# A two-layer graph attention kernel: the first lookup table in node order, its loads and stores on ScalarE, the second layer's indices from VectorE

## The chip, the cores and the metric

One core of a Trainium2 chip. The time is the device time of one execution in microseconds (us), as the median of several runs. TensorE is PE in the profile, VectorE DVE, ScalarE ACT, GpSimd POOL, SyncE SP.

## The reference

Eight batches of 2048 nodes with 64 values each, and one adjacency matrix of 2048 x 2048 integers. Layer 1 has four heads, layer 2 one.

```python
mask = graph + jnp.eye(N, dtype=graph.dtype) > 0
h = jnp.einsum('bnc,hdc->bhnd', x, Wh)
out_h = _gat_layer(h, mask[None, None], bh[None, :, None, :])   # scores h h^T, masked, softmax, times h, plus b
cat = jnp.transpose(out_h, (0, 2, 1, 3)).reshape(B, N, H * D)
z = jax.nn.leaky_relu(cat, negative_slope=0.2)
h2 = jnp.einsum('bnk,dk->bnd', z, Wo)
out2 = _gat_layer(h2, mask[None], bo)
z2 = jax.nn.leaky_relu(out2, negative_slope=0.2)
mu = jnp.mean(z2, axis=-1, keepdims=True)
var = jnp.mean(jnp.square(z2 - mu), axis=-1, keepdims=True)
out = (z2 - mu) * jax.lax.rsqrt(var + LN_EPS) * gamma + beta
x = _layernorm(x + out, axis=-1)
```

The adjacency is sparse: the chance of an edge between two nodes falls with both numbers, so nodes with low numbers have many neighbours and the others few.

## The kernel before, in words

The kernel uses the sparsity. The first 32 nodes (`HUB`) are computed against all nodes. The other 2016 are put into 168 sets (`NS`) of 12 (`SET`), and for each set a list of at most 128 neighbours of any of its members is made. A set is then worked on with the 128 rows of its list only, which GpSimd gathers from a table in device memory (`indirect_dma_start`, L817): `table1` holds x of all batches (2080 bytes a node), `table2` the layer-2 values. A node's number alone does not say where it stands in a table: the members of a set stand next to each other, 12 rows a set, and member 0 of the sets comes in blocks of 24 (`FLIP`) in reversed order of the blocks. One tile `index` (128 list places x 168 sets) holds row numbers for both tables.

**First stage.** SP loads the adjacency in pieces of 120 rows x 1024 (10 sets; a load of 10 rows, at times cut in two, for the members 0, L694, and one of 110 rows for the rest, L695). GpSimd turns a piece into zeros and ones (L700). TensorE multiplies by powers of two, so that bit k of a column says whether member k of the set has that neighbour; VectorE adds the column's row number (`number`, L731): key = bits x 2048 + number. Then the largest 128 keys of each set are searched eight at a time (`pick`, L758 and L760), transposed, and cut into row number (`index`, L788) and bits (`mask`, L801). An entry that is no neighbour gets 2048 added, which the gather leaves out as out of bounds.

Beside this a loop over 16 tiles of 128 nodes (`for i in range(NB)`, L979) works on the hub nodes: `load_x(i + 4)` loads a later tile of x (two transfers, L474; the tiles 0 to 3 on ScalarE's queue, the rest on SP's), `save_x(i)` stores tile i to `table1` (L479, on ScalarE's queue, one transfer for each run of rows that the table's order leaves together, 33 for all tiles), `hub_scores(i)` makes scores on TensorE (L615), subtracts the mask on VectorE (L618) and takes the exponential on ScalarE (L620), `turn_x(i + 1)` transposes the next tile (ScalarE copies it to `xT`, L608), `hub_values(i - 1)` multiplies by the values (L631). At i = 2 and 6 the keys of the first 60 sets are made, and from i = 6 on four steps of `pick` follow in each iteration. Each queue works in the order in which its instructions are recorded; a wait of a transfer on ScalarE's queue holds ScalarE's later instructions too.

The transfers that SP and ScalarE issue are counted by eight semaphores, given out in turn over both queues in the common order of the recorded program. A transfer that takes a semaphore again waits until that semaphore's earlier transfer has landed, if its engine has not seen that yet.

**Second stage.** A loop over 84 pairs of sets (`for i in range(-4, NG + 3)`, L1125) runs layer 1: gather five pairs ahead (L1153, L817), transpose (L538), scores (L847), mask (L852), exponential, values (L872), normalise (L879, L880), bias and leaky ReLU (L544, L549), projection for layer 2 (L906, L911), rows of `table2` stored (L920, L923). Small jobs for later are put in between by iteration; the list `ahead_of_second` holds jobs that prepare layer 2 (clearing buffers, `link` at L1060), one every second iteration from i = 60 on.

**Third stage.** Layer 2 over groups of four sets: gather from `table2` with the same `index`, transposes, scores, values (L1275), two layer norms, and the stores of the result (L1358).

Of the kernel before, what the change touches and what calls it, by code (L numbers as in the profile page):

```python
# [31 lines left out]
I32 = mybir.dt.int32  # L32
# [4 lines left out]
OP = mybir.AluOpType  # L37
# [7 lines left out]
HUB = 32  # L45
SET = 12
# [313 lines left out]
def fast_kernel(ctx: ExitStack, tc: tile.TileContext, x, adj, Wh, bh, Wo, bo, gamma, beta, out, flag):  # L360


    nc = tc.nc
    B, N, C = x.shape
    H, D, _ = Wh.shape
    P = 128
# [7 lines left out]
    NS = (N - HUB) // SET  # L374
# [7 lines left out]
    HALFN = N // 2  # L382
    NHB = (NS + S10 - 1) // S10
    FLIP = 24
    REST = HUB + NS
    assert NS * SET == N - HUB and NS % FLIP == 0 and FLIP % 8 == 0 and HUB == 32 and Q * HUB == P

    const = ctx.enter_context(tc.tile_pool(name="const", bufs=1))
# [15 lines left out]
    def rows_tile(name):  # L404
        return rowp.tile([P, Q, PW], F32, tag="rows", name=name)
# [11 lines left out]
    share = [const.tile([P, n], F32, name=f"share{k}") for k, n in enumerate([HALFN, HALFN, HALFN, 512, 512, 2 * 264])]  # L417
# [10 lines left out]
    table1 = dram.tile([N, ROW], F32, name="table1")  # L428
# [7 lines left out]
    ownh = const.tile([P, Q * HUB], F32, name="ownh")  # L436
    keysi = const.tile([P, NS], I32, name="keysi")
    index = const.tile([P, NS], I32, name="index")
    mask = const.tile([P, NS, M], U8, name="mask")
    maskh = const.tile([P, NB, HUB * H], U8, name="maskh")  # L440
    maskt = const.tile([P, NHB + 1, HUB], U8, name="maskt")
# [8 lines left out]
    xrow = {}  # L450

    def flipped(s0, ns):

        runs = []
        while ns:
            n = min(ns, FLIP - s0 % FLIP)
            runs.append((s0, HUB + (NS // FLIP - 1 - s0 // FLIP) * FLIP + s0 % FLIP, n))
            s0, ns = s0 + n, ns - n
        return runs

    def in_order(table, a, b):

        sets = table[HUB:, :].rearrange("(s k) c -> k s c", k=SET)
        runs = [(0, HUB, table[:HUB, :])]
        runs += [(n0, n0 + n, sets[0, s0:s0 + n]) for s0, n0, n in flipped(0, NS)]
        runs += [(HUB + k * NS, HUB + (k + 1) * NS, sets[k]) for k in range(1, SET)]
        return [(max(a, n0), min(b, n1), dst[max(a, n0) - n0:min(b, n1) - n0]) for n0, n1, dst in runs if max(a, n0) < min(b, n1)]

    def load_x(i):
        t = xrow[i] = rows_tile(f"x{i}")  # L470
        nc.vector.memset(t[:, :, 0:PW:PW - 1], 1.0)
        for p in range(2):
            queue = nc.scalar if i < 4 else nc.sync
            queue.dma_start(out=t[:, :, 1 + p * D:1 + (p + 1) * D],  # L474
                                in_=x[p::2, i * P:(i + 1) * P, :].rearrange("q n c -> n q c"))

    def save_x(i):
        for a, b, dst in in_order(table1, i * P, (i + 1) * P):
            nc.scalar.dma_start(out=dst, in_=xrow[i][a - i * P:b - i * P].rearrange("n q c -> n (q c)"))  # L479

    NCH = HALFN
    in_round = [min(FIRST, NS - FIRST * r) for r in range(NR)]
    pieces = [(r, t, m) for r in range(NR) for t in range((in_round[r] + S10 - 1) // S10) for m in range(2)]
    load_x(0)
    hubraw = [early.tile([HUB, NCH], I32, tag="raw", name=f"hubraw{k}", bufs=3) for k in range(2)]
    for k in range(2):
        nc.sync.dma_start(out=hubraw[k], in_=adj[0:HUB, k * NCH:(k + 1) * NCH])
    for r in range(2):
        nc.sync.dma_start(out=wnat[half(r)], in_=Wh.rearrange("h d c -> d h c"))
    nc.sync.dma_start(out=wos, in_=Wo)  # L490
    load_x(1)
    with nc.allow_non_contiguous_dma(reason="a few hundred bytes of parameters"):
        nc.gpsimd.dma_start(out=bhp, in_=bh.rearrange("(q e) d -> (e d) q", e=2))
# [12 lines left out]
    for k in range(SET):  # L506
        nc.gpsimd.affine_select(out=d, in_=d, pattern=[[0, 3], [-1, 10]], base=-10 * k, channel_multiplier=1,
                                compare_op=OP.not_equal, fill=float(1 << k))
    number = share[2].bitcast(U16).rearrange("p (h c) -> p h c", h=2)
    nc.gpsimd.iota(number[:, :, :HUB // 2], [[1, 2], [2, HUB // 2]], base=0, channel_multiplier=0)  # L510
    nc.gpsimd.iota(number[:, :, HUB // 2:REST // 2].rearrange("p h (b c) -> p h b c", c=FLIP // 2),
                   [[SET, 2], [-FLIP * SET, NS // FLIP], [2 * SET, FLIP // 2]], base=HUB + SET * (NS - FLIP), channel_multiplier=0)
    nc.gpsimd.iota(number[:, :, REST // 2:].rearrange("p h (k c) -> p h k c", k=SET - 1),
                   [[SET, 2], [1, SET - 1], [2 * SET, NS // 2]], base=HUB + 1, channel_multiplier=0)
    load_x(2)
    load_x(3)

# [296 lines left out]
    def gather(table, s, layer, new):  # L814
        t = rows[layer, s] = new(f"g{layer}_{s}")
        bound = {} if layer == 2 and s < 36 else dict(bounds_check=N - 1, oob_is_err=False)
        nc.gpsimd.indirect_dma_start(out=t.rearrange("n q c -> n (q c)"), out_offset=None, in_=table,  # L817
                                     in_offset=bass.IndirectOffsetOnAxis(ap=index[:, s:s + 1], axis=0), **bound)

    def own_rows(m):  # L820

        t = held["x", m] = work.tile([P, 2 * GM], F32, tag="xo", name=f"xo{m}", bufs=2)
        to = t.rearrange("c (s q k) -> c s q k", s=4, q=Q)
        nc.gpsimd.tensor_copy(to[:, :, :, 1:], xT[:, :, REST:].rearrange("c q (k s) -> c s q k", s=NS)[:, 4 * m:4 * m + 4])
        n0 = flipped(4 * m, 4)[0][1]
        nc.gpsimd.tensor_copy(to[:, :, :, 0], xT[:, :, n0:n0 + 4].rearrange("c q s -> c s q"))
# [187 lines left out]
    for g in range(LOOK - 2):  # L1014
        for j in range(2):
            gather(table1, 2 * g + j, 1, rows_tile)
# [19 lines left out]
    sets = [list(range(4 * u, min(4 * u + 4, NS))) for u in range(NU)]  # L1036
    bd = [t.rearrange("p (k q n) -> p k q n", k=4, q=Q) for t in (share[2][:, :512], share[2][:, 512:], share[4])]
    es2 = [t.rearrange("p (b k n) -> p b k n", b=2 * Q, k=4) for t in share[:2]]
# [4 lines left out]
    def spread_own(u):  # L1043

        w = len(sets[u])
        for p in range(2):
            src = own[half(p), :, sets[u][0] * SET:(sets[u][0] + w) * SET]
            nc.scalar.copy(bd[u % 3][half(p), :w, :, 16 * p:16 * p + SET], src.rearrange("c q (k n) -> c k q n", k=w))
# [6 lines left out]
    def clear_ends():  # L1055
        for k in range(2):
            nc.vector.memset(esh[k][:, Q * 2 * HUB:], 1.0)
        nc.vector.memset(es2[0][:, :, :, 24:], 1.0)

    def link():  # L1060
        nc.vector.tensor_scalar(index[:, :36], index[:, :36], N - 1, None, OP.bitwise_and)
        nc.vector.tensor_scalar(linked, mask.rearrange("p s (k h) -> p s k h", h=H)[:, :, :, 0], 0.0, None, OP.is_equal)

    W2 = D + 2
# [46 lines left out]
    def hub_step(k, sp):  # L1111
# [3 lines left out]
        if 0 < k <= NHB + 1:  # L1115
            hub_values2(k - 1)

    ahead_of_second = ([clear_own] + [lambda t=t: nc.vector.memset(t, 0.0) for t in bd + es2] + [clear_ends, link] +
                       [lambda u=u: spread_own(u) for u in range(3)])

    ready, done = FIRST, FIRST
# [3 lines left out]
    for i in range(-4, NG + 3):  # L1125
# [15 lines left out]
        if 0 <= i + 2 < NG:  # L1141
            t = held["T", 1, i + 2] = work.tile([P, 2, 512], F32, tag="xTg", name=f"xTg{i + 2}", bufs=3)
# [11 lines left out]
        if NG - LOOK <= i < NG - 1:  # L1154
            for j in range(2):
                k = 2 * (i - NG + LOOK) + j
                hub_block(k, rows_tile(f"gh{k}"))
        if i + 6 < NG and i % 2 == 0 and i >= -2:
            own_rows((i + 6) // 2)
        if i >= 60 and i % 2 == 0 and ahead_of_second:  # L1160
            ahead_of_second.pop(0)()
        if i % 2 == 0 and 0 <= (i - 30) // 2 <= NV:
            load_own((i - 30) // 2)
# [252 lines left out]
    k = 9  # L1416
    for u in range(-3, NU + 5):
# [12 lines left out]
        if 0 <= u < NU:  # L1430
            a = u % 2
# [10 lines left out]
        if 0 <= u + 1 < NU:  # L1442
            turn_scores(u + 1)
            a = (u + 1) % 2
# [49 lines left out]
```

## Time and profile before

| | us |
|---|---|
| median of 3 timed runs | 1020.71 (1017.41 to 1027.33) |
| the profiled execution, its own time | 892.68 |
| its span from first to last instruction | 890.9 |
| first exponential of the tile loop (L620) starts | 46.42 |
| last exponential of the tile loop starts | 122.31 |
| first gather of layer 1 (L817) starts | 130.98 |
| last gather of layer 1 starts | 576.0 |
| first gather of layer 2 starts | 611.1 |

The profiled execution was shorter than the timed runs by 128 us. The profile's page gives busy times, which overlap; the chain that ended last is followed back from the last instruction, step by step to what released it. In a row of a timeline come the start, the time it took, the engine, the line, what is written and read, and in brackets how long the engine had stood idle and what ended that. "ACTq" and "SPq" are instructions that issue a transfer; their time is that of the issue, not of the data.

### The profile page before, as it was taken

The numbers are of one execution on the slowest core, as the hardware profiler recorded it, in microseconds if no ns is written. First come the engines' busy times: TensorE is split into PE (matmuls) and PEld (weight loads), VectorE is DVE, ScalarE is ACT, GpSimd is POOL, SyncE is SP. The second block draws the span as 40 slices with busy tenths as digits, with TensorE's granted clock in tenths as the row PEclk, the third lists the DMA queues.
The fourth block names the chain that finished last, engine by engine and source line by source line (L and its number), as shares of the span: only waits on it lengthen the run. The fifth ranks groups of instructions, "written<-read, shape, count | busy, mean of one in ns | idle before, by whom it ended". The sixth has DMA issues, their size and how long they took to land.

```text
span 890.9 us, 42340 instructions
## 1 busy us (share of the span) xinstructions
PE 729.4 (82%) x18079; PEld 644.2 (72%) x18079; DVE 592.2 (66%) x1358; ACT 502.6 (56%) x1038; POOL 503.2 (56%) x709
## 2 busy tenths in 40 slices
PE   2266657899999999999999999986998888888830
PEld 2254545788889889889898888875887787887720
DVE  2136962788978778775556566552249989998882
ACT  2032313566656666666666666662567778787720
POOL 5234338386445456556566666504777777777501
PEclk9998977999999999999999999999799999999965
DMA  7377746344223334444444444435975666766510
GB/s 118 117 215 187 208 151 167 91 141 112 79 78 91 95 97 128 121 124 133 127 136 131 129 125 126 115 97 151 301 219 164 191 181 185 204 187 182 172 45 25
DMA packets 82419, 125.70 MB, mean 141 GB/s; under 512 B 35440, under 2 KB 51672, under 8 KB 82222
## 3 DMA queue, kind: packets, MB, share of 16 engines
q0 software_dynamic: 27168, 69.09, 28.4%
q1 hardware_dynamic: 48088, 48.36, 18.6%
q10 hardware_dynamic: 6966, 5.45, 2.3%
q8 instruction: 145, 2.38, 1.1%
q14 instruction: 52, 0.43, 0.1%
HBM read 124.98 MB, written 18.48 MB: 161 GB/s over the span
## 4 chain that ended last, share of the span: by engine, by line
PE 52%; DVE 16%; DMA 13%; issue 6%; SPq 5%; ACT 4%; POOL 2%; ACTq 0%; POOLq 0%; DVEq 0%
PE o L872 10%; PE s L847 9%; PE bank L538 7%; DMA raw<-in_adj_dram 6%; PE cat L832 5%; PE cat L557 3%; PE o L889 3%; SPq L1358 3%; DMA rows<-table,index 3%; PE cat L906 3%; PE t L538 2%; PE cat L916 2%; DVE st_s L1309 2%; DVE y_s L1329 2%; DMA table<-x 2%
## 5 line engine op out<-in xcount | busy, mean ns | idle before, releaser
L817 POOL DMA_INDIRECT g<-table,index x168 | 178.0, 1060 | 163.5 <-PE o L872 133.7
L817 POOL DMA_INDIRECT rows<-table,index x168 | 178.1, 1060 | 55.5 <-issue 23.2
L852 DVE TENSOR_TENSOR e<-s,mask 128x768 f32<-128x768 f32 x84 | 80.3, 955 | 87.7 <-PE s L847 87.6
L544 ACT ACTIVATE z<-cat,bhp 128x192 f32<-128x192 f32 x168 | 61.4, 416 | 80.3 <-PE cat L557 80.3
L872 PE MATMUL o<-g,e 128*64 128x65 f32 x2688 | 100.5, 226 | 4.7 <-issue 4.5
L538 PE MATMUL bank<-ident,g 128*128 128x128 f32 x672 | 101.5, 275 | 0.7 <-DVE keysi L786 0.6
L1390 ACT COPY xts<-t 128x1024 f32<-128x1024 f32 x84 | 81.1, 1010 | 33.1 <-PE t L538 31.5
L872 PEld LDWEIGHTS o<-g,e 128*64 128x64 f32 x2688 | 87.3, 139 | 16.1 <-issue 6.2
L847 PE MATMUL s<-y,xTg 64*64 64x48 f32 x5376 | 97.6, 221 | 1.3 <-DVE share L731 1.2
L847 PEld LDWEIGHTS s<-y,xTg 64*64 64x64 f32 x5376 | 86.9, 135 | 15.6 <-issue 15.1
L538 PE MATMUL t<-ident,rows 128*128 128x128 f32 x672 | 86.3, 279 | 10.1 <-DMA rows<-table,index 9.4
L1144 ACT COPY xTg<-bank 128x512 f32<-128x512 f32 x168 | 90.2, 596 | 0.6 <-PE bank L538 0.6
L538 PEld LDWEIGHTS t<-ident,rows 128*128 128x128 f32 x672 | 76.5, 144 | 14.2 <-issue 6.3
L700 POOL TENSOR_SCALAR a<-raw 120x1024 bf16<-120x1024 int32 (+1 forms) x34 | 37.8, 1113 | 81.2 <-DMA raw<-in_adj_dram 55.2
L538 PEld LDWEIGHTS bank<-ident,g 128*128 128x128 f32 x672 | 80.9, 142 | 3.3 <-DVE keysi L786 1.2
L838 ACT COPY y<-cat 128x384 f32<-128x384 f32 x80 | 41.0, 513 | 73.5 <-PE o L889 36.2
L859 ACT ACTIVATE e<-e,shifts 128x768 f32<-128x768 f32 x84 | 81.0, 964 | 2.4 <-DVE e L852 2.4
L879 DVE RECIPROCAL rall<-o 64x8 f32<-64x8 f32 x168 | 34.4, 205 | 51.4 <-PE o L872 50.1
L832 PE MATMUL cat<-xo,gram 128*128 128x192 f32 x320 | 65.9, 328 | 0.7 <-issue 0.7
L880 DVE TENSOR_TENSOR osb<-o,rall 128x512 f32<-128x512 f32 x84 | 58.1, 692 | 2.9
L620 ACT ACTIVATE e<-e,shifts 128x1024 f32<-128x1024 f32 x16 | 18.4, 1149 | 73.2 <-DVE e L618 36.1
L832 PEld LDWEIGHTS cat<-xo,gram 128*128 128x128 f32 x320 | 53.3, 201 | 1.6 <-issue 1.4
(193 smaller groups left out, 1446.1 us busy)
## 6 DMA issues: line engine op xcount, KB each, us to landing
raw<-in_adj_dram SPq DMA_DIRECT2D x32, 440.0 KB
table<-xb SPq DMA_DIRECT2D x22, 256.0 KB
xr_s<-table SPq DMA_DIRECT2D x21, 256.0 KB
table<-rowt SPq DMA_DIRECT2D x166, 24.4 KB
xb<-in_x_dram SPq DMA_DIRECT2D x168, 22.0 KB
out_dram<-y_s SPq DMA_DIRECT2D x160, 22.0 KB
x<-in_x_dram SPq DMA_DIRECT2D x24, 128.0 KB
g<-table,index POOLq DMA_INDIRECT x168
```

The source lines that it names most:

```text
L538: nc.tensor.transpose(tp[:, q * P:(q + 1) * P], rows[:, q, 1:1 + P], ident)
L544: nc.scalar.activation(z[:, hp], cat[:, :, hp * n:(hp + 1) * n], AF.Identity, bias=bhp[:, hp:hp + 1], scale=1.0)
L817: nc.gpsimd.indirect_dma_start(out=t.rearrange("n q c -> n (q c)"), out_offset=None, in_=table, in_offset=bass.IndirectOffsetOnAxis(ap=ind ...
L832: nc.tensor.matmul(cat[:, k, 2 * GM:2 * GM + n], gram[:, g % 2 * 2 + k, :], held["x", g // 2][:, :n], start=True, stop=True)
L838: nc.scalar.copy(held["y", g // 2][:, :n, g % 2 * 2:g % 2 * 2 + 2], cat[:, :, 2 * GM:2 * GM + n].rearrange("p a n -> p n a"))
L847: nc.tensor.matmul(sp[half(r), p, (q * 2 + j) * M:(q * 2 + j + 1) * M], xt[half(p), j, q, half(r)], y[half(p), (j * Q + q) * M:(j * Q + q ...
L852: nc.vector.tensor_tensor(e[:, :16 * M].rearrange("p (a q n) -> p a q n", a=2, q=Q), sp[:, :, :8 * M].rearrange("p a (q n) -> p a q n", q= ...
L859: nc.scalar.activation(e[:, :16 * M], e[:, :16 * M], AF.Exp, bias=shifts[:, 0:1], scale=1.0)
L872: nc.tensor.matmul(op[half(p), j, o0:o0 + K1], e[:, c0:c0 + 64], rw[j][:, q, sums(p)], start=True, stop=True)
L880: nc.vector.tensor_tensor(osb, v[:, :, :, 1:K1], r.unsqueeze(3).to_broadcast([P, 4, 2, D]), OP.mult)
L1144: nc.scalar.copy(t[:, k, :], bank[k])
L1390: nc.scalar.copy(t, tp)
```

## The change

`table1` is stored in the order of the node numbers, each tile of 128 nodes by one transfer on ScalarE's queue; `in_order` is gone. `number` is then the node's number itself, made by one iota. `index` therefore points into `table1` only, and layer 2, whose `table2` keeps the order of the sets, gets a tile `index2`, which VectorE works out from `index` by comparing the node number with the bounds of member classes and blocks (25 instructions on 128 x 168 integers). These stand as five jobs at the head of `ahead_of_second`, which now starts at i = 50. All tiles of x are loaded from ScalarE's queue.

```diff
     index = const.tile([P, NS], I32, name="index")
+    index2 = const.tile([P, NS], I32, name="index2")
...
-    def in_order(table, a, b):
-
-        sets = table[HUB:, :].rearrange("(s k) c -> k s c", k=SET)
-        runs = [(0, HUB, table[:HUB, :])]
-        runs += [(n0, n0 + n, sets[0, s0:s0 + n]) for s0, n0, n in flipped(0, NS)]
-        runs += [(HUB + k * NS, HUB + (k + 1) * NS, sets[k]) for k in range(1, SET)]
-        return [(max(a, n0), min(b, n1), dst[max(a, n0) - n0:min(b, n1) - n0]) for n0, n1, dst in runs if max(a, n0) < min(b, n1)]
-
     def load_x(i):
         t = xrow[i] = rows_tile(f"x{i}")
         nc.vector.memset(t[:, :, 0:PW:PW - 1], 1.0)
         for p in range(2):
-            queue = nc.scalar if i < 4 else nc.sync
-            queue.dma_start(out=t[:, :, 1 + p * D:1 + (p + 1) * D],
+            nc.scalar.dma_start(out=t[:, :, 1 + p * D:1 + (p + 1) * D],
                                 in_=x[p::2, i * P:(i + 1) * P, :].rearrange("q n c -> n q c"))
 
     def save_x(i):
-        for a, b, dst in in_order(table1, i * P, (i + 1) * P):
-            nc.scalar.dma_start(out=dst, in_=xrow[i][a - i * P:b - i * P].rearrange("n q c -> n (q c)"))
+        nc.scalar.dma_start(out=table1[i * P:(i + 1) * P, :], in_=xrow[i].rearrange("n q c -> n (q c)"))
...
-    nc.gpsimd.iota(number[:, :, :HUB // 2], [[1, 2], [2, HUB // 2]], base=0, channel_multiplier=0)
-    nc.gpsimd.iota(number[:, :, HUB // 2:REST // 2].rearrange("p h (b c) -> p h b c", c=FLIP // 2),
-                   [[SET, 2], [-FLIP * SET, NS // FLIP], [2 * SET, FLIP // 2]], base=HUB + SET * (NS - FLIP), channel_multiplier=0)
-    nc.gpsimd.iota(number[:, :, REST // 2:].rearrange("p h (k c) -> p h k c", k=SET - 1),
-                   [[SET, 2], [1, SET - 1], [2 * SET, NS // 2]], base=HUB + 1, channel_multiplier=0)
+    nc.gpsimd.iota(number, [[1, 2], [2, HALFN]], base=0, channel_multiplier=0)
...
-                                     in_offset=bass.IndirectOffsetOnAxis(ap=index[:, s:s + 1], axis=0), **bound)
+                                     in_offset=bass.IndirectOffsetOnAxis(ap=(index if layer == 1 else index2)[:, s:s + 1], axis=0), **bound)
...
+    node, late_sets, blocks = [share[5][:, k * NS:(k + 1) * NS].bitcast(I32) for k in range(3)]
+
+    def node_steps():
+        nc.vector.tensor_scalar(node, index, N - 1, None, OP.bitwise_and)
+        nc.vector.tensor_scalar(late_sets, node, float(REST), None, OP.is_ge)
+        nc.vector.tensor_scalar(blocks, node, float(HUB + FLIP), None, OP.is_ge)
+        nc.vector.scalar_tensor_tensor(index2, late_sets, float(SET * (NS - FLIP)), index, OP.mult, OP.add)
+
+    def count(into, first, step, js):
+        for j in js:
+            nc.vector.scalar_tensor_tensor(into, node, float(first + step * j), into, OP.is_ge, OP.add)
+
+    def set_order():
+        nc.vector.scalar_tensor_tensor(index2, late_sets, float(1 - NS * SET), index2, OP.mult, OP.add)
+        nc.vector.scalar_tensor_tensor(index2, blocks, float(-2 * FLIP * SET), index2, OP.mult, OP.add)
+        nc.vector.tensor_scalar(blocks, node, float(HUB), None, OP.is_ge)
+        nc.vector.tensor_scalar(node, node, float(SET - 1), float(SET * (NS - FLIP) - HUB * (SET - 1)), OP.mult, OP.add)
+        nc.vector.tensor_tensor(node, node, blocks, OP.mult)
+        nc.vector.tensor_tensor(index2, index2, node, OP.add)
+
     def link():
-        nc.vector.tensor_scalar(index[:, :36], index[:, :36], N - 1, None, OP.bitwise_and)
+        nc.vector.tensor_scalar(index2[:, :36], index2[:, :36], N - 1, None, OP.bitwise_and)
...
-    ahead_of_second = ([clear_own] + [lambda t=t: nc.vector.memset(t, 0.0) for t in bd + es2] + [clear_ends, link] +
+    ahead_of_second = ([node_steps, lambda: count(late_sets, REST, NS, range(1, 6)), lambda: count(late_sets, REST, NS, range(6, SET - 1)),
+                        lambda: count(blocks, HUB, FLIP, range(2, NS // FLIP)), set_order, clear_own] + [lambda t=t: nc.vector.memset(t, 0.0) for t in bd + es2] + [clear_ends, link] +
                        [lambda u=u: spread_own(u) for u in range(3)])
...
-        if i >= 60 and i % 2 == 0 and ahead_of_second:
+        if i >= 50 and i % 2 == 0 and ahead_of_second:
```

## The prediction

> **What bounds the kernel now.** I read the page first (busy shares, the 40 slices, the chain), then busy time by stretch, then the timelines of ACT, DVE and SP over the first 165 us, because all three named edits act there or on what it leaves behind. From the page:
>
> ```profile
> span 890.9 us, 42340 instructions
> PE 729.4 (82%) x18079; PEld 644.2 (72%) x18079; DVE 592.2 (66%) x1358; ACT 502.6 (56%) x1038; POOL 503.2 (56%) x709
> ```
>
> By stretch (us, then busy us of each engine, granted clock, DMA share, GB/s):
>
> ```profile
> 36.00:76.00 40.00, 22.03 (x432) 16.98 (x432) 9.92 (x13) 11.34 (x14) 17.33 (x63) 1.00 0.78 213
> 76.00:131.00 55.00, 34.10 (x655) 26.37 (x653) 47.04 (x125) 14.11 (x17) 19.29 (x42) 0.84 0.59 171
> 131.00:390.00 259.00, 242.00 (x6208) 215.15 (x6212) 194.90 (x519) 158.28 (x362) 151.28 (x227) 0.97 0.40 111
> ```
>
> Up to 76 us no engine is busy; the stretch waits. From 76 to 131 us VectorE works 47 of 55 us. From 131 us on TensorE works 94%. So a gain can only come from the first 76 us (the second stretch then starts earlier at its old length), and work added to VectorE after 131 us costs only where it makes TensorE wait. In the first stretch ScalarE stands before its first exponentials:
>
> ```profile
> 36.14 10.17 ACTq L479 DMA_DIRECT2D table<-x  x5
> 46.42 1.15 ACT L620 ACTIVATE e<-e,shifts 128x1024 f32<-128x1024 f32 x1 [21.61 <-DMA table<-x]
> ...
> 51.40 1.15 ACT L620 ACTIVATE e<-e,shifts 128x1024 f32<-128x1024 f32 x1 [3.36 <-DMA table<-x]
> ```
>
> The operand of the first exponential was done at 31.07 (VectorE, L618, 29.84 + 1.23). The bracket is the idle time and what ended it: five stores of one x tile, queued ahead on ScalarE. The chain of waits says what the last of the five waited for:
>
> ```profile
> 41.04 4.95 DMA raw<-in_adj_dram
> 46.01 2.89 DMA table<-x
> ```
>
> The wait is not for the tile: in the built program the transfers of SP and ACT take eight semaphores in turn in one common order, so each is issued only when the eighth before it has landed. An adjacency load of 110 rows issued at 41.04 lands at 45.99 and frees the store. After that the loop of 16 tiles turns at 4.17 us (exponential 1.15, xT copy 0.57, scores 1.1, subtract 1.23) until VectorE's keys and top-8 searches fill it:
>
> ```profile
> 76.36 2.47 DVE L731 SCALAR_TENSOR_TENSOR share<-pk,share 32x1024 f32<-32x1024 f32 x2 [2.19 <-PE pk L742]
> ```
>
> In the long stage an iteration takes 5.00 us, and VectorE has room in it. Two places show how much: at 473.67 three extra instructions (0.77 us) before L549, and at 550 the step `link`.
>
> ```profile
> 476.23 0.27 DVE L1051 MEMSET share<- 128x256 f32 x1
> 476.54 0.50 DVE L1053 COPY share<-ownh 64x128 f32<-64x128 f32 x2
> ...
> 477.91 0.27 DVE L920 TENSOR_TENSOR rowt<-cat,bob 96x128 f32<-96x128 f32 x1
> 478.67 0.96 DVE L852 TENSOR_TENSOR e<-s,mask 128x768 f32<-128x768 f32 x1 [0.48 <-PE s L847]
> ...
> 550.10 1.28 POOL L951 TENSOR_TENSOR xb<-xb,bet 128x512 f32<-128x512 f32 x1 [3.52 <-DMA table<-rowt]
> 550.15 1.27 DVE L1061 TENSOR_SCALAR index<-index 128x36 int32<-128x36 int32 x1
> 551.34 1.31 DVE L1062 TENSOR_SCALAR maskh<-mask 128x2016 uint8<-128x2016 uint8 x1
> ...
> 553.57 0.50 ACT L838 COPY y<-cat 128x384 f32<-128x384 f32 x1 [3.02 <-DVE rowt L920]
> ...
> 554.55 0.92 PE L557 MATMUL cat<-otb,whT 64*64 64x96 f32 x16 [1.96 <-ACT otb L896]
> ```
>
> In the first, L920 ends 4.51 us after its iteration's L852 instead of 3.39 (406.34 to 409.73), and the next L852 still comes 5.00 us later: 1.1 us of delay are free. In the second L920 is 2.4 us late, ScalarE's copy L838 waits for it, TensorE stands 1.96 us, and the two iterations from 547.67 to 561.27 take 13.60 instead of 10.0.
>
> **What the Trainium skill says.** DMA: Bandwidth & Descriptors, section Issuing engines are not separate DMA queues: transfers of ScalarE and SyncE run on the same 16 engines, so a change of queue saves issue time only. I take the moved loads' data time as unchanged; no view here contradicts it. Same page, Anatomy of one DMA — SWDGE (gpsimd) path: a fixed cost of about 2 us per transfer, mostly the receipt, stated for transfers that GpSimd issues. The trace has the same for SP's: 10 rows of 4 KB issued at 15.44 take 1.93 us in the chain. Same page, Why a DMA increments its semaphore by 16 and not by 1: a transfer runs on the largest number of engines up to 16 that divides its rows, so 24 rows use 8 and 128 rows 16; no view shows engines singly. SBUF — State Buffer, section Who interferes with whom: VectorE in a two-port mode (tensor_scalar can enter it) and GpSimd block each other for a whole instruction. The trace agrees: L1061 on 36 columns took 1.27 us beside POOL's L951, where L788 on 60 columns took 0.19.
>
> **The change part by part.** The profiled execution took 892.68 us around a span of 890.9; the median of the timed runs is 1020.71, 128 us more, and nothing in the profile places that. I work on the profiled execution and carry the difference over in us.
>
> *Stores.* 33 stores become 16. The first tile's five become one, the second's four become one. *Loads of x4 to x15.* 24 issues leave SP and go to ScalarE, each pair ahead of that iteration's store and exponential. SP's next adjacency loads are no longer behind them; ScalarE goes from 41 to 48 issues (33 + 8, then 16 + 32), in the loop three an iteration. At the median 0.48 us for a load (L474) and 0.36 for a store (L479) that is 1.3 us, and ScalarE idles 2.55 us between its xT copy and the next exponential: hidden, as long as no semaphore holds them.
>
> Now the semaphores, by the built program's order. Iteration 0: the two loads of x4 stand where the first two stores stood and wait for the same landings (36.12 and 39.42, from the stores' issue at 36.14 and 39.44); the store stands where the third stood, issued at 40.03. First exponential about 40.5 for 46.42: 6 us earlier. Iteration 1: the loads of x5 wait for the 10-row load issued at 41.92, and the store for the 110-row load issued at 42.48; with 6 us for that (49.20 to 55.20 in the chain) it lands at 48.7, exponential about 49.1 for 51.40: 2.3 left. Iteration 2: the loads of x6 wait for piece 4's 110 rows, free to issue at 46.0 instead of 46.66, landing 5.5 us later; exponential about 52.5 for 55.58. Iteration 3, after the keys' 2.5 us on VectorE: 58.7 for 61.68. With turns of 4.17 the second keys then start near 73.4 for 76.36, **3.0 us earlier**. What can give it back: without the x loads SP's pieces come closer together, the common order has 26 transfers in the four iterations from x8 to x12 (17 before), and eight in flight at 6.5 an iteration allow a landing time of 8/6.5 x 4.17 = 5.1 us; pieces land in 4.6 to 6 us here. So one or two of the loads x8 to x10 should hold ScalarE for about a microsecond. I take half: **-1.5 us** at the first gather. Bounds: -13 (ScalarE never held: the first exponential at 31.1, the seventh six turns and one pair of keys later, and the second keys 2.2 us behind it as now: 31.1 + 25.0 + 2.5 + 2.2 = 60.8; I put 63, an estimate, because the twelfth piece, converted at 66.36 now, has to be in by then) and +9 (0.75 us lost in each of 12 iterations).
>
> *From 76 to 131 us.* VectorE's list is unchanged; ScalarE waits 3.3 us in each turn for VectorE, which covers three issues. 0. *Iota.* One for three (0.15 + 0.31 + 1.74 us before), and POOL then waits 2.75 us for the adjacency anyway: 0. *Layer-1 gathers.* Same 168, same rows in another order, issued five iterations ahead; TensorE's transposes have no wait for them worth a row: 0. *Layer-2 gathers* read the same table through `index2`, with rows in the order of nodes instead of sets; they make 2.8% of the chain, 25 us, so a tenth longer would be 2.5 us. I take 0 and keep 0 to +2.5.
>
> *VectorE's 25 instructions at i = 50, 52, 54, 56, 58* (4, 5, 5, 5, 6), all on 128x168 and each on the result before it. Nearest row: the 128x168 int32 TENSOR_TENSOR at 119.49, its successor at 119.85, so 0.36 us each: 1.44, three times 1.80, 2.16; 9.0 us in all. They stand ahead of L549, as `link` does: behind them L549, L911, L920, then ScalarE's L838 and L896, then TensorE's L557. With 1.1 us free each time: 0.34 + 3 x 0.70 + 1.06 = **+3.5 us**. Bounds: 0 (TensorE slower than in this profile would leave more room) and +10 (two tensor_scalar instructions blocked 1.1 us by POOL's L951, and half the price of `link`'s second slow iteration each time). The rest of that list (`clear_own` to `spread_own`) keeps its iterations from i = 60.
>
> Sum: -1.5 + 3.5 = +2.0, 894.7 for 892.68; on the median **1022.7**.
>
> **Rivals.** *A, within 1%* (the above). *B, faster:* adjacency transfers were the pacer and fewer transfers in the common order let both loads and stores flow. For it: 50% of the chain up to 76 us are adjacency transfers, 12.8% stores. Against: the first six pieces go one by one to 34 us, untouched. Its time is the lower bound of the first stretch with the index work hidden: -13, 1007.7. *C, slower:* ScalarE's queue becomes the bound. Its exponential and xT copy, and so TensorE's scores and VectorE's subtract, stand behind loads that wait for adjacency pieces. It decides once pieces land later than about 5.1 us in the 4.17-us turns, 6.1 in turns of 4.95. For it: landings of 5.74 at 92.02 and 6.00 at 49.20. Against: VectorE's pace leaves 3.3 us from 78 us on. Price +9 with +3.5 from VectorE: 1033.2. *That the change doesn't do what it says:* the moved loads could wait for the same landings that SP waited for, so that the first stretch keeps its length and only the index work is seen, +3.5: 1024.2, inside A.
>
> **How the numbers follow.** A 0.45, B 0.30, C 0.25. One per cent, 10 us, is about what a measurement of this kernel tells from no change (the three runs span 1017 to 1027). A's own range is -4 to +8, 1017 to 1029. The range reaches to B and C and a little past, 1005 to 1036. B and C are each taken as whole beyond 1%, A as whole within it: faster 0.30, same 0.45, slower 0.25.
>
> **What would show it.** Right: first exponential near 40.5, second near 49, the second keys near 73 to 76, first gather (130.98 before) within 129 to 131; the iterations at i = 50 to 58 at 5.3 to 6.1 us with ScalarE's L838 copy ended by VectorE. Wrong: a first gather before 122 (B), or ScalarE's exponentials ended by transfers of x over several microseconds in many tiles (C), or any difference after 615 us.

## The result and the profile after

The change takes 1031.58 us at the median, the kernel before 1021.99 on the same chip (16 runs each): ratio 1.008, 95% interval 1.0058 to 1.0103, so 8.2 us slower, between 5.9 and 10.5. The forecast was 1022.7 with "within 1%" as the likeliest outcome; that is where it fell, at the slow edge (0.8%, and the interval reaches just past 1%), and the sum of the prediction (+2.0) is too small by some 6 us.

The profiled execution of the change took 1023.52 us. That of the kernel before took 892.68 us, which is what this kernel takes on a faster chip, as the first experiment shows; so the two pages are not subtracted from each other, and stretches are compared only where a run allows it. The page of the changed kernel begins:

```profile
span 1021.7 us, 42335 instructions
PE 772.5 (76%) x18079; PEld 667.6 (65%) x18079; DVE 605.3 (59%) x1383; ACT 507.1 (50%) x1038; POOL 499.5 (49%) x707
```

VectorE has 25 instructions more, as written, and 13.1 us more busy time; 10.5 of these are the 25 (mean 0.42 us). The timeline of ScalarE in the tile loop after the change, in the same columns as the one shown of before (the exponential is now line 607, loads of x line 466, stores line 470):

```profile
37.47 4.50 ACTq L466 DMA_DIRECT2D x<-in_x_dram  x2
42.25 0.35 ACTq L470 DMA_DIRECT2D table<-x  x1
42.72 1.15 ACT L607 ACTIVATE e<-e,shifts 128x1024 f32<-128x1024 f32 x1 [19.63 <-DMA x<-in_x_dram]
...
49.21 0.93 ACTq L466 DMA_DIRECT2D x<-in_x_dram  x2
50.82 0.35 ACTq L470 DMA_DIRECT2D table<-x  x1
51.21 1.15 ACT L607 ACTIVATE e<-e,shifts 128x1024 f32<-128x1024 f32 x1 [6.88 <-DMA x<-in_x_dram]
```

The stores no longer hold the first exponential (42.72 for 46.42), but the loads do: two of them take ScalarE's queue 4.50 us, because the second waits for an earlier transfer, the adjacency load of 110 rows that SP issued at 35.89. At the second tile nothing is left of the gain (51.21 for 51.40). VectorE's second keys, at 77.50, come no earlier than before (76.36 in the profile shown of before, 77.55 in a second one):

```profile
77.50 2.46 DVE L718 SCALAR_TENSOR_TENSOR share<-pk,share 32x1024 f32<-32x1024 f32 x2 [2.19 <-PE pk L729]
```

The chain of waits between 30 and 80 us names the loads outright; two of its pieces show how long a load took whose semaphore the next transfer on ScalarE's queue needed:

```profile
51.26 7.07 DMA x<-in_x_dram
58.36 5.50 DMA x<-in_x_dram
```

The first gather starts at 130.53, for 130.98 before. In the long stage the timeline around the third job of the index work (i = 54) shows where time goes (L907 makes rows of layer 2, L825 and L883 are ScalarE's copies, L544 the projection, L859 the values):

```profile
464.69 2.49 DVE L1057 SCALAR_TENSOR_TENSOR share<-share 128x168 int32<-128x168 int32 x5
467.10 0.55 DVE L536 SCALAR_TENSOR_TENSOR z<-z 128x384 f32<-128x384 f32 x1
467.74 0.28 DVE L907 TENSOR_TENSOR rowt<-cat,bob 96x128 f32<-96x128 f32 x1
468.10 0.50 ACT L825 COPY y<-cat 128x384 f32<-128x384 f32 x1 [3.01 <-DVE rowt L907]
468.49 0.54 ACT L883 COPY otb<-o 128x192 f32<-128x192 f32 x2
469.09 0.56 PE L544 MATMUL cat<-otb,whT 64*64 64x96 f32 x16 [1.64 <-ACT otb L883]
469.58 1.15 PE L859 MATMUL o<-g,e 128*64 128x65 f32 x32
```

VectorE spends 2.49 us on five instructions, the leak (L536) and the rows (L907) come so much later, ScalarE's copy L825 waits 3.01 us for the rows, and TensorE stands 1.64 us before L544. The iterations go by the start of VectorE's weighing (L839): the one with the job takes 5.88 us (462.06 to 467.94), the next one 6.69; without the index work such iterations take 5.5 us in the mean (88.70 us for 16, in a run below). TensorE's pauses before L544 after the jobs at i = 52, 54, 56 and 58 are 1.47, 1.64, 1.17 and 2.03 us, 6.3 in sum; after the short job at i = 50 there is none.

### The profile page after: what moved, and what is told of

It reads as the page before. It is cut to its first block, busy times and chain, and to the rows that moved or that the text cites. A ratio compares the mean times of both kernels' runs of the same rounds, so it can differ in the third digit from the quotient of the medians.

```text
span 1021.7 us, 42335 instructions
## 1 busy us (share of the span) xinstructions
PE 772.5 (76%) x18079; PEld 667.6 (65%) x18079; DVE 605.3 (59%) x1383; ACT 507.1 (50%) x1038; POOL 499.5 (49%) x707
## 4 chain that ended last, share of the span: by engine, by line
PE 54%; issue 12%; DVE 10%; DMA 8%; ACT 7%; another core or an unknown queue 4%; SPq 2%; POOL 1%; ACTq 0%; DVEq 0%; POOLq 0%
PE s L834 9%; PE o L859 9%; PE bank L525 6%; PE t L525 5%; PE cat L819 5%; DMA raw<-in_adj_dram 4%; DMA x<-in_x_dram 3%; PE cat L544 3%; PE o L876 3%; PE cat L893 2%; ACT xts L1398 2%; PE bank L1264 2%; PE bank L1253 2%; SPq L1366 2%
## 5 line engine op out<-in xcount | busy, mean ns | idle before, releaser
L804 POOL DMA_INDIRECT rows<-table,index x168 | 173.7, 1034 | 144.5 <-PE o L1283 86.4
L839 DVE TENSOR_TENSOR e<-s,mask 128x768 f32<-128x768 f32 x84 | 80.3, 956 | 97.5 <-PE s L834 96.4
L834 PE MATMUL s<-y,xTg 64*64 64x48 f32 x5376 | 116.6, 222 | 8.7 <-issue 5.7
L834 PEld LDWEIGHTS s<-y,xTg 64*64 64x64 f32 x5376 | 100.8, 134 | 28.2 <-issue 22.5
L525 PE MATMUL t<-ident,rows 128*128 128x128 f32 x672 | 93.0, 283 | 11.1 <-issue 8.4
L859 PE MATMUL o<-g,e 128*64 128x65 f32 x2688 | 99.6, 226 | 1.9 <-issue 1.7
L859 PEld LDWEIGHTS o<-g,e 128*64 128x64 f32 x2688 | 86.9, 139 | 12.8 <-issue 2.8
L825 ACT COPY y<-cat 128x384 f32<-128x384 f32 x80 | 41.1, 513 | 80.7 <-DVE rowt L907 48.2
L1253 PE MATMUL bank<-xts,share 128*32 128x128 f32 x1344 | 55.1, 283 | 30.3 <-issue 19.1
L687 POOL TENSOR_SCALAR a<-raw 120x1024 bf16<-120x1024 int32 (+1 forms) x34 | 37.9, 1116 | 79.8 <-DMA raw<-in_adj_dram 42.7
L1253 PEld LDWEIGHTS bank<-xts,share 128*32 128x32 f32 x1344 | 38.8, 112 | 45.0 <-issue 40.5
L1283 PE MATMUL o<-rows,share 128*32 128x65 f32 x2688 | 55.0, 224 | 11.5 <-issue 6.3
```

Source lines behind the costliest of these rows:

```text
L525: nc.tensor.transpose(tp[:, q * P:(q + 1) * P], rows[:, q, 1:1 + P], ident)
L834: nc.tensor.matmul(sp[half(r), p, (q * 2 + j) * M:(q * 2 + j + 1) * M], xt[half(p), j, q, half(r)], y[half(p), (j * Q + q) * M:(j * Q + q ...
L839: nc.vector.tensor_tensor(e[:, :16 * M].rearrange("p (a q n) -> p a q n", a=2, q=Q), sp[:, :, :8 * M].rearrange("p a (q n) -> p a q n", q= ...
L859: nc.tensor.matmul(op[half(p), j, o0:o0 + K1], e[:, c0:c0 + 64], rw[j][:, q, sums(p)], start=True, stop=True)
L1253: nc.tensor.matmul(sp[q * 32:(q + 1) * 32, k, :], bd[u % 3][:, k, q, :], xt[:, s % 2, q, :], start=True, stop=True, tile_position=(0, q * 32))
L1283: nc.tensor.matmul(op[t * 32:(t + 1) * 32, f, k * W2 + p:k * W2 + p + K1], e[:, 2 * q + p, k, :], rw[:, q, sums(p)], start=(a == 0 and k = ...
```

## Experiments

Each was timed beside the kernel before on the same chip, in five rounds; "us" is the ratio applied to the median of before. Two places are read in every profile: the start of the first gather, and the 16 iterations from VectorE's weighing of pair 45 to that of pair 61, in which all of the index work lies.

| run | ratio (interval) | us against before | before there | first gather | 16 iterations |
|---|---|---|---|---|---|
| before (profile shown) | | | | 130.98 | 81.81 |
| before again | 0.9998 (0.9977 to 1.0018) | 0 | 894.6 | 131.98 | 82.15 |
| single stores and index work | 1.0077 (1.0040 to 1.0114) | +6.9 | 894.6 | 127.90 | 96.00 |
| moved loads alone | 1.0083 (1.0060 to 1.0105) | +7.4 | 894.6 | 135.01 | 81.79 |
| index work alone | 1.0136 (1.0091 to 1.0180) | +12.2 | 894.6 | 132.03 | 92.65 |
| the change again | 1.0142 (1.0102 to 1.0183) | +12.7 | 893.8 | 135.13 | 95.55 |
| two at a time, ahead of the leak | 1.0031 (1.0007 to 1.0055) | +2.8 | 893.8 | 129.73 | 83.92 |
| two at a time, behind the rows | 1.0027 (1.0007 to 1.0048) | +2.4 | 893.8 | 131.36 | 82.12 |
| the same, loads on SP | 0.9990 (0.9963 to 1.0017) | -0.9 | 893.8 | 127.49 | 82.06 |
| the change (profile shown) | 1.0080 (1.0058 to 1.0103) | +8.2 | 1022.0 | 130.53 | 94.82 |
| change without index work | see text | | 1025.6 | 132.39 | 88.70 |
| single stores without index work | see text | | 1025.6 | 128.17 | 89.24 |
| stores and loads on SP | 0.9980 (0.9957 to 1.0003) | -2.1 | 1025.6 | 129.07 | 89.41 |
| the same, loads earlier | 1.0070 (1.0051 to 1.0089) | +7.1 | 1021.1 | 135.45 | 87.60 |

One profile is one execution: runs of one kernel on one chip spread over 7 to 17 us, and the first gather of programs that do not differ up to there (the change, and the three runs that move or drop only the index work) lies at 130.53, 135.13, 129.73, 131.36 and 132.39.

**The kernel before, again, and the change, again.** No edit.

> The kernel before, once more, to have a profiled execution of it in the condition in which it is timed: the profile shown of it took 892.68 us, its timed runs 1021.99 at the median, and the change's profile 1023.52. If the 129 us belong to the execution and not to the kernel, this profile takes about 1020 and shows, like the changed kernel's, a stretch of some 40 us in which TensorE stands at the start of layer 2, and iterations of layer 1 near 5.4 us instead of 5.00. If the changed kernel's slow start of layer 2 is its own, this profile shows TensorE standing there for a few us only. Ratio to the kernel before 1.000 either way.

> The change itself once more, beside the parts that were run apart (single stores with the index work +6.9 us, moved loads +7.4, index work alone +12.2 against before's 894.6). If the parts act in different places, its profile has the first gather between those of the parts run apart (127.90 and 135.01), near 130.5, and the iterations at i = 50 to 58 as in the run of the index work alone, some 11 us longer in sum: +9 to +11 us in all. If the moved loads add to the index work, +14 to +20.

The kernel before took 894.7 us on this chip, with no long pause at the start of layer 2. The change, run again on one more chip, takes 907.2, and has no such pause either. So the 128 us that the prediction could not place go with the chip: the kernel before runs at 894 us on two chips and at 1021 to 1026 on three other occasions. Whether it is the chip itself or its state at the time, no run tells. In the profiles the difference lies mostly in layer 2, whose gathers take 312.3 us from first to last in the profile of the change and 227.8 when it ran again, and little in layer 1. But the price of the change differs too: +12.7 here (interval +9.1 to +16.4, so both ranges of the expectation, +9 to +11 and +14 to +20, remain possible) for +8.2 there. The 16 iterations (95.55 for 81.81 to 82.15) hold all of it, +13.6. Part of the expectation was that the first gather be near 130.5; it was 135.13, within the spread above.

Why the same work costs twice as much here, the timeline of TensorE in this run shows, at the job of i = 56:

```profile
474.92 0.56 PE L544 MATMUL cat<-otb,whT 64*64 64x96 f32 x16 [1.75 <-ACT otb L883]
475.41 1.94 PE L859 MATMUL o<-g,e 128*64 128x65 f32 x32
```

The pause is much as on the other chip, 1.75 us, but the 32 matmuls behind it take 1.94 us for 1.15. Busy time by stretch (us, five engines, granted clock, DMA share, GB/s) of this run, and below it that of the first profile of the change behind its pause at 469:

```profile
474.10:475.10 1.00, 0.18 (x8) 0.18 (x12) 0.61 (x1) 0.77 (x3) 0.00 (x0) 1.00 0.21 53
475.10:479.00 3.90, 3.90 (x60) 3.56 (x57) 1.56 (x4) 2.53 (x5) 1.29 (x2) 0.56 0.15 36
```

```profile
470.00:475.00 5.00, 5.00 (x133) 4.49 (x131) 2.30 (x7) 3.30 (x8) 3.55 (x4) 1.00 0.36 98
```

Here the granted clock falls to 0.56 for 3.9 us behind the pause, which loses 3.9 x 0.44 = 1.7 us. In this run it does so behind all four long jobs (L859 at 2.00, 2.00, 1.94 and 2.00 us). Its five pauses come to 8.1 us (0.69, 1.61, 1.95, 1.75, 2.12), and with four falls to 14, for the 13.6 found, when a fall is taken at 1.5 us: in the run of the index work alone (below) two iterations behind a pause of 1.94 us differ by that, 7.94 us with a fall and 6.44 without. In the first profile of the change no L859 behind a pause takes more than 1.15 us, the pause of 2.03 us included, and the pauses alone are the cost. The Trainium skill (TensorE: Matmul & The Clock Gate, section What's actually happening) has the clock at half after an idle window of about 3.4 us; here it fell behind a pause of 1.61 us too (the L859 of 2.00 us at i = 52), so the measurement decides.

**The parts of the change alone.** First the single stores in node order with the index work, the loads back on SP:

```
-            nc.scalar.dma_start(out=t[:, :, 1 + p * D:1 + (p + 1) * D],
+            (nc.scalar if i < 4 else nc.sync).dma_start(out=t[:, :, 1 + p * D:1 + (p + 1) * D],
```

> The change with the x loads of tiles 4 to 15 back on SP's queue; the table in node order, its single stores and the index work stay. Theory 1 (the index work on VectorE costs about 6 us and nothing else costs anything): as slow as the change, +6 to +8 against before. Theory 2 (ScalarE's queue, held by the moved loads, costs most): within 2 us of before, with the second keys on VectorE at 72 to 74 us instead of 77.50. Theory 3 (rows in node order make the gathers of layer 1 slower): as slow as the change, with the iterations of layer 1 longer from the first gather on.

Then before with the moved loads alone:

```
-            queue = nc.scalar if i < 4 else nc.sync
+            queue = nc.scalar
```

> The kernel before with only the x loads of tiles 4 to 15 moved to ScalarE's queue; 33 stores, the table in the order of sets and no index work. Theory 1: within 2 us of before. Theory 2: 5 to 8 us slower than before, since ScalarE then carries 33 stores and 32 loads, all in the order of the shared semaphores; first gather at 134 to 138 us instead of 130.98. Theory 3: within 2 us of before.

And before with the index work alone (`node_steps`, `count`, `set_order` and their five jobs from i = 50, as in the change):

> The kernel before with only the 25 instructions of the index work at i = 50 to 58 on VectorE; what they work out is read by nothing. Theory 1: +5 to +8 us against before, the ten iterations from the first of them about 6 us longer than without. Theory 2: 0 to +3. Theory 3: 0 to +3. By the sum of the prediction: +3.5.

The index work costs +12.2, of it 10.7 in the 16 iterations; theory 1 named the place and undersized it for these chips. The same pause has two prices in this run's timeline of TensorE (L558 is the projection, L873 the values there):

```profile
451.80 0.56 PE L558 MATMUL cat<-otb,whT 64*64 64x96 f32 x16 [1.94 <-ACT otb L897]
452.29 1.15 PE L873 MATMUL o<-g,e 128*64 128x65 f32 x32
...
463.95 0.92 PE L558 MATMUL cat<-otb,whT 64*64 64x96 f32 x16 [1.94 <-ACT otb L897]
464.80 2.00 PE L873 MATMUL o<-g,e 128*64 128x65 f32 x32
```

Behind 1.94 us at full clock one time, at half the next: two of the four long jobs are followed by a fall in this run, all four in the two other runs of bursts on such chips, none in the profile of the result. So the length of the pause alone does not decide it, and what does was not tested; that two falls less are 3 us less than the +13.6 and +14.0 of those runs agrees with it as the source of the difference. Theory 2 is right on its own terms as well: moved loads alone cost, with the first gather 3.0 us later than in the run of before again. In that run ScalarE's queue shows both kinds of transfer ahead of the first exponential:

```profile
37.27 4.40 ACTq L474 DMA_DIRECT2D x<-in_x_dram  x2
41.80 7.45 ACTq L479 DMA_DIRECT2D table<-x  x5
49.37 1.15 ACT L620 ACTIVATE e<-e,shifts 128x1024 f32<-128x1024 f32 x1 [27.18 <-POOL a L700]
```

The timed +7.4 (the two medians differ by 5.4) is more than these 3 us; the rest was not found in its one profile, which at 896.8 us was among its fastest executions. Single stores, with loads on SP, bring the first gather to 127.90, 4 us ahead of before, and the first exponential to 37.2. So the first stretch is a draw of two parts: stores -4, loads +4. Theory 3 falls: the 16 iterations take as long with the table in either order once the index work is hidden (below).

**Place or number of the index instructions.** The 25 are issued two at a time from i = 46:

```
+        for _ in range(2 if i >= 46 else 0):
+            if order_steps:
+                order_steps.pop(0)()
         if 0 <= i - 1 < NG:
             leak(held["z", i - 1])
```

> The change, with the 25 instructions of the index work two at a time in 13 iterations from i = 46, still ahead of the leak (line 536 of the changed kernel). By the prediction's rule of 1.1 us free in each iteration: 0.94 us each, nothing left of their cost, -1 to +1 us against before. If what stands ahead of the leak delays TensorE's projections of the iteration after it in full: 13 times 0.7 to 0.9, +8 to +11. If it is the burst of five and the clock that falls after it: in between, +3 to +6.

And the same three lines behind `keep_rows(i - 3, pr)`:

> The change, with the same instructions two at a time from i = 46, but issued behind VectorE's last piece of the iteration (the rows of layer 2, line 907 of the changed kernel), where VectorE idles 1.6 us before it weighs the next scores. If the place in VectorE's order is what costs: nothing of the index work is left, and what remains is the first stretch, -2 to +1 us against before. If the 25 instructions cost by being there (VectorE's and GpSimd's common port, gathers issued later): as slow as the run that has them ahead of the leak, +8 or more.

The 16 iterations fall from 95.55 to 83.92 and 82.12. Two at a time ahead of the leak leave 2 us of 13.6, and behind the rows nothing is left (82.12 for 81.81 and 82.15 before). So the burst is the larger part of the cost, but the place is not free: in the run ahead of the leak most of the iterations with two instructions take 5.2 to 5.5 us instead of 5.00, some 4 us in sum, and only because the three long ones of before (5.68, 5.26 and 5.92) are absent does the sum rise by no more than 2. Five at once behind the rows were not run. Both totals still lie above before (+2.8 and +2.4, at least +0.6); their profiles (first gather at 129.73 and 131.36) do not show where. How the instructions disappear is seen in the timeline of the second:

```profile
459.33 0.28 DVE L907 TENSOR_TENSOR rowt<-cat,bob 96x128 f32<-96x128 f32 x1
459.53 0.32 DVE L1057 SCALAR_TENSOR_TENSOR index<-share,index 128x168 int32<-128x168 int32 x1
459.70 0.52 ACT L825 COPY y<-cat 128x384 f32<-128x384 f32 x1 [0.60 <-PE o L876]
459.88 0.44 DVE L1058 TENSOR_SCALAR share<-share 128x168 int32<-128x168 int32 x1
460.00 1.15 PE L834 MATMUL s<-y,xTg 64*64 64x48 f32 x64
460.09 0.55 ACT L883 COPY otb<-o 128x192 f32<-128x192 f32 x2
460.97 0.53 PE L544 MATMUL cat<-otb,whT 64*64 64x96 f32 x16
461.26 0.96 DVE L839 TENSOR_TENSOR e<-s,mask 128x768 f32<-128x768 f32 x1 [0.93 <-PE s L834]
```

They stand where VectorE would wait for the scores. The same rows give the time that a delay ahead of the leak may take for nothing: the rows L907 end at 459.61 and ScalarE takes L825 at 459.70, for TensorE's L876 and not for them; its otb copy ends at 460.64, and TensorE takes L544 at 460.97, behind its scores. That is 0.1 + 0.3 = **0.4 us**. The run ahead of the leak agrees: its two instructions put the leak off by 0.66 to 0.69 us in six iterations, and TensorE then stands 0.2 us, so 0.4 to 0.5 were free:

```profile
438.78 0.56 PE L544 MATMUL cat<-otb,whT 64*64 64x96 f32 x16 [0.23 <-ACT otb L883]
```

On the chip of the result the scores took 1.45 us (466.00 to 467.45 in the first profile) for 1.15, which makes it 0.7. On that chip the four long jobs put the leak off by 2.41, 2.41, 2.21 and 2.68 us, 9.7 in sum (from the start of the job to that of L536); less 4 x 0.7 that is 6.9, for pauses of 6.3.

**Loads on SP as well.** The last run with the loads back on SP:

> As the run with the index work behind VectorE's last piece, and the x loads of tiles 4 to 15 back on SP's queue: single stores, node order, index work hidden. If place is what costs, the gain of the single stores alone is left, first gather near 127.9 for 132.0, -4 us or a little more against before, and 3 us or so faster than with the loads on ScalarE. If the index work costs wherever it stands: +5 to +8.

The first gather is at 127.49, 3.9 us ahead of the run with the loads on ScalarE, as expected; the total is 3 us better than that run's and not to be told from before (-3.3 to +1.5). So of the 4 us gained at the first gather the total time shows at most 3. In this one profile layer 1 takes 450.1 us from its first to its last gather, for 445.3 in the run with the loads on ScalarE, and nothing in the edit explains that.

**Without the index work.**

> The single stores in node order alone, with the x loads of tiles 4 to 15 on SP's queue; the index work is left out, so that layer 2 gathers as many rows from the same table, but by the numbers of nodes, other rows than it should. Where the index work behind VectorE's last piece was free: as the run with it, -1 to 0 us against before, and the 4.5 us gained at the first gather must be lost elsewhere. Where it cost 3 us there: -4 us, as the first gather has it.

> The change without its 25 instructions of index work; layer 2 gathers as many rows from the same table, but by the numbers of nodes, other rows than it should. If the index work at its place is the whole loss: -2 to +1 us against before, some 12 us faster than the change. If the moved loads cost as they do beside 33 stores: +4 to +7.

Both took some 7340 us in all: on the rows gathered, the kernel's own test of its sums (`in_limits`) sent it into its second path, which computes everything anew, so their totals say nothing. The stages of the first path can be read, on a chip where before takes 1025.6. The change without the index work needs 88.70 us for the 16 iterations; with it 94.82: **+6.1 us**, on two chips on which the kernel before takes nearly the same time (1022.0 and 1025.6). The four profiles on such chips in which the index work is left out or stands behind the rows have 87.60 to 89.41, so the difference lies between 5.4 and 7.2. Between the two runs, single stores with loads on SP are ahead by 4.2 us at the first gather, by 4.1 at the last gather of layer 1 (595.21 and 599.26), by 5.0 at the first of layer 2 (629.69 and 634.70) and by 3.2 at the last (942.09 and 945.30): here the gain of the first stretch is carried through.

**ScalarE's queue emptied.** Stores on SP too, and in a second run the loads of tiles 4 to 7 earlier and the others eight tiles ahead:

```
-        nc.scalar.dma_start(out=table1[i * P:(i + 1) * P, :], in_=xrow[i].rearrange("n q c -> n (q c)"))
+        nc.sync.dma_start(out=table1[i * P:(i + 1) * P, :], in_=xrow[i].rearrange("n q c -> n (q c)"))
```

> The run with the index work behind VectorE's last piece and the x loads on SP, with the single stores on SP's queue too, so that ScalarE issues nothing after the loads of tiles 0 to 3 and its exponentials wait for no transfer but that of their own tile. If ScalarE's waits in its queue pace the tile loop: second keys at 64 to 70 us instead of 73.1, first gather at 122 to 125, -4 to -9 us against before. If the adjacency pieces pace it, or SP's queue, now with all transfers: second keys at 73 to 77, -1 to +3.

```
-    more(6)
+    more(1)
+    for i in range(4, 8):
+        load_x(i)
+    more(5)
...
-            load_x(i + 4)
+            load_x(i + 8)
```

> The run with stores and loads on SP's queue and the index work behind VectorE's last piece, with the x loads of tiles 4 to 7 issued behind the first adjacency piece (SP idles there from 5.3 to 16.8 us) and the others eight tiles ahead instead of four. In the run without this the fourth tile's transfer was issued at 51.27, behind ten adjacency pieces, and the exponential of tile 4 came at 62.7. If that is what holds the tile loop now: tiles 3 to 6 at turns of 4.17 us behind the first keys, second keys at 65 to 68 us instead of 73.2, first gather at 121 to 124 instead of 129.1, 5 to 7 us more gained, -8 to -10 us against before. If the adjacency pieces pace the second keys: 72 to 74 us, -2 to -3 as without.

With ScalarE's queue empty the first three exponentials start at 29.62, 33.72 and 37.90, the pace of 4.17 us that the prediction's rival B assumed. The second keys still come at 73.2, as with the stores on ScalarE (73.1): the wait moved to the loads of x, which SP issues behind ten adjacency pieces (the first at 51.27; tile 4's exponential at 62.7). The total is 2.1 us below before, interval -4.4 to +0.3: the best of the versions run, and not shown to be faster. Loading earlier was meant to remove that wait and added a worse one, on VectorE:

```profile
58.89 0.07 DVE L464 MEMSET x<- 128x8 f32 x1 [21.38 <-DMA x<-in_x_dram]
58.96 1.23 DVE L605 TENSOR_TENSOR e<-sh,maskh 128x1024 f32<-128x1024 f32 x1
```

`load_x` begins with a memset of its tile by VectorE. There are ten such buffers, so tile 10 takes that of tile 0, whose store SP issued only at 53.87; the memset of 0.07 us waits and the subtraction of the tile loop stands behind it for 21.38 us. (The bracket names a load of x because another of the semaphores that the memset waits for moved last; the store's was complete just before.) Second keys at 82.5, first gather at 135.45, +7.1.

## Why the prediction was right or wrong

*The forecast*, case A, holds: within 1%, 1022.7 for 1031.6, inside the range. It holds because its range was wider than its sum was good: of +2.0, both terms were too kind. And there is luck in it: where it ran again, the same change measured +1.4% (1.0 to 1.8), which is outside case A; the falls of the clock behind the pauses, which make most of the difference, were not in the prediction's sum.

*VectorE's instructions, +3.5*: the term that failed. On chips like that of the result it measured +6.1, and +10.7 to +14.0 on the two others. The failing step is "1.1 us of delay are free". It was read from the three extra instructions at 473.67, because the next L852 still came 5.00 us later. But a delay of L920 reaches ScalarE's copies and TensorE's projection in the following iteration. Behind the L852 at 478.67, which was shown there, the same profile of before has:

```profile
479.26 0.56 PE L557 MATMUL cat<-otb,whT 64*64 64x96 f32 x16 [0.66 <-ACT otb L896]
...
484.54 0.96 DVE L852 TENSOR_TENSOR e<-s,mask 128x768 f32<-128x768 f32 x1 [1.61 <-PE s L847]
```

TensorE stands 0.66 us, the next L852 comes 5.87 us later, and the cost was in that. What is free is 0.4 us (0.7 where the scores are slower). `link`'s second iteration of 7.87 us had shown the same at full size, and the prediction used it for the upper bound only. Smaller was the price of one instruction: 0.36 taken, 0.42 measured. The bounds, 0 to +10, held the result. "TensorE slower would leave more room" was right as well.

*The first stretch, -1.5*: about 0. Five executions of the new first stage have the first gather at 131.8 in the mean, three of the old one at 131.7. The mechanism was right, order of semaphores included, but the landings were guessed too short, by 2 us at the first two tiles and 4 in sum from the third on: exponentials predicted at 40.5, 49.1, 52.5 and 58.7 came at 42.7, 51.2, 56.7 and 62.8, and the second keys at 77.5 for 73.4. Two of the moved loads took 7.07 and 5.50 us to land; the 5.1 us that the prediction named as the limit were exceeded in the very first tiles, where it feared for tiles 8 to 10.

*Rival C* (ScalarE's queue becomes the bound) is therefore true as a mechanism: the moved loads cost some 4 us at the first gather. It did not decide, because the single stores gained as much. *Rival B* needed a ScalarE that is never held; even with its queue emptied the loop was held by the loads of x behind the adjacency, and the second keys came no earlier than 73.2. *That the change does nothing in the first stretch*, priced at +3.5, came closest in kind, for another reason.

*Costs taken at nothing*: the single iota and the gathers. The keys now hold the node's number, so within one pattern of bits a list is sorted by node number; `index2` translates each entry but leaves that order, and layer 2 reads its rows of `table2` in it, as the prediction says. Neither is seen in the time: 227.8 us between the first and last gather of layer 2 in the change, 228.3 in before again, both on chips of the faster kind.

*The unplaced 128 us* were a difference of chips. Carrying the sum over in us took the price of the index work to be the same on both kinds; it was not (+6.1 and +10.7 to +14.0), mostly because the clock fell behind the bursts in three profiles and not in that of the result. One slip carries nothing: by the row shown TensorE works 93% from 131 to 390 us (242.00 of 259.00), not 94.

Of +8.2, the index work is +6.1 and the first stretch about 0; the 2 us that are left lie within the interval, and no run places them.

## What to carry to other kernels

In a pipeline over iterations, follow a delay to where TensorE next waits for it before calling it free: look at the iteration after the one that looks unharmed. Small jobs for an engine with idle time belong behind its last piece that others wait for, and a few at a time; here four bursts of five in front of it, which put that piece off by 9.7 us, cost about 6, and some 1.5 us more each time TensorE's clock fell after the pause. And a queue that is relieved of one kind of transfer and given another has not been relieved: 17 stores less and 24 loads more came to nothing.

## What the runs showed of the hardware

- The same kernel takes 894 us on some chips and 1021 to 1026 on others. On the slower ones 168 gathers of layer 2 take 308 to 314 us for 228 to 230, and layer 1's scores 116.6 us for 97.2, in matmuls of the same mean duration:

```profile
L834 PE MATMUL s<-y,xTg 64*64 64x48 f32 x5376 | 116.6, 222 | 8.7 <-issue 5.7 <-DVE share L718 1.2
```

```profile
L834 PE MATMUL s<-y,xTg 64*64 64x48 f32 x5376 | 97.2, 220 | 1.1 <-DVE share L718 1.1
```

  The first is the profile of the result, the second the change again on another chip; columns are busy us, mean ns, and idle time before with what ended it. These matmuls have one mean duration and follow each other more slowly in the first; why is not known.
- Twelve pauses of TensorE of 1.3 to 2.2 us on two chips (three runs) were followed in ten cases by a fall of the granted clock, to 0.56 over 3.9 us where it is shown above; the two without were of 1.33 and 1.94 us. None of four pauses of 1.2 to 2.0 us on the chip of the result was followed by one.
